# A hand-ordered schedule for two layers of spectral convolution: list offsets of the pairs, the transform back and the first transform

## Chip, cores and metric

One NeuronCore of a Trainium2 chip runs the whole program. The metric is the device time of one execution in microseconds (us), of which smaller is better.

## What is computed

The input `x` is four images of 256 x 256 positions with 64 channels, in float32. Layer 0 is a block with a Fourier branch and a depthwise convolution; layer 1 takes a moving average along the rows and adds a filtered spectrum. Cut to what matters:

```
# layer 0
h  = ln(x) @ w_te + b_te                       # 64 -> 128 channels
F  = fft2(h, axes=(1, 2))
fc = gelu(concat(real(F), imag(F)) @ w_fc + b_fc)
sp = real(ifft2(fc[..., :128] + 1j * fc[..., 128:], axes=(1, 2)))
x1 = x + sp @ w_tp + b_tp
h2 = ln(x1) @ w_fe + b_fe
d  = gelu(depthwise_conv_3x3(h2, w_dw) + b_dw)
x2 = x1 + d @ w_fp + b_fp
# layer 1, along the second axis, for each channel
trend = moving_average(x2, 25)
out   = trend + irfft(einsum(rfft(x2 - trend)[:128], w_real + 1j * w_imag))
```

## The kernel before

Transforms are matmuls with tables of cosines and sines. Layer 0 runs as three streams, and each stream is cut into small operations with short names. The names below are those of the lists; the numbers are lines of the kernel.

**First transform** (`forward_h`, 32 chunks for each image): `fl` loads a chunk (L564, L569), `fq fr fR fm` and `fM fA fB fC fp` are the layer norm's statistics, `fx` scales (L410), `fa fb` fold halves on VectorE (L582, L602), `fh0 fh1` on GpSimd (L609), `y0 y1` are the matmuls (L615), `yt0 yt1` copy out on ScalarE (L633) and write `y_d` to HBM (L649).

**Pairs** (`spectral`, 65 pairs of rows for each image): `x` (L725) is a transform on TensorE that reads `yb` (L680, from `y_d`), `xs` (L740) its copy on ScalarE, `m0 m1` (L750) the channel mix on TensorE, `gc0 gc1` (L764) a copy on ScalarE, `b0 b1` (L770) sum and difference on VectorE, `g0 g1` (L775) the gelu on ScalarE, `p0 p1` (L781) a fold on GpSimd, `z` (L805), `zs` (L813), `w` (L823) and `zt` (L833) a projection, a copy, a transposition and a copy. **Transform back:** `u` (L856, TensorE), `us` (L873, ScalarE), `uc` and `uf` (L887, L888, L907, L920, VectorE), the last with the write of `u_d` (L896). One period has two pairs and one step back.

**Convolution** (`convolution`, 32 chunks for each image): `UL`/`ul` load `uc` from `u_d` (L976, and L985, L997 for an image's first chunk), `c0` (L990) corrects a column, `s` (L1041) is the last transform, `r0 r1` (L1054, L1062) the residual, `cq` to `cp` the second layer norm's statistics (lines as for the first), then transpositions `t`, row sums `T` (L1124 to L1132, GpSimd), the convolution's matmuls `gm gh em eh` (L1166, L1180), its combination, gelu, projection and `st` (L1322).

The order in which TensorE, VectorE, ScalarE and GpSimd get their instructions is written out by hand (`in_order`, L1531). The DMA queue on SyncE is ordered by the framework. Each number `n` is one **period**; the list that belongs to it is walked from the left, and an entry `op:k` asks for operation `op` up to index `n + k` (the stream's own count; pairs count `2 * (n - S0) + k`, `S0` being 35):

```python
    def period(n):
        if any(n - k in chunk_at for k in range(7)):
            names = FULL if n < B * FWD + 4 else MIXED if n < CONV_FROM else CONV
        else:
            names = SPECTRUM
```

`SPECTRUM` has the first transform and the pairs, `FULL` all three streams, `MIXED` the pairs and the convolution, `CONV` the convolution alone. `do(op, index)` first pulls whatever the operation depends on, in the order of that table (`FOLLOWS`), so an index that runs ahead of the last list is made up at that place, one operation after the other:

```python
        for k in range(done.get(op, -1) + 1, index + 1):
            for other, at in EARLY.get(op, ()) if k < LATE_CHUNKS else ():
                do(other, k + at)
            for other, at in follows.get(op, ()):
                do(other, k + at)
```

The convolution's chunks get their periods from `chunk_at` (L1540): image 0 has 71 to 102, image 1 104 to 135, image 2 136 to 167, image 3 169 to 200. `FULL` begins at 71 with `b0:2` and ends with 131; `MIXED` ends with 169. Before an image's first chunk `UL` pulls the last steps back of that image. In `SPECTRUM` a forward chunk's root is a power on GpSimd (L383); in `FULL` it shares a chain of ten small steps with a convolution chunk (`cA` to `cp`, L354 to L397, `rstd_c`), taken in the order ScalarE, GpSimd, ScalarE and so on. After layer 0, layer 1 multiplies with matrices made at the start (L1504).

Of the kernel before, what the change touches and what calls it, by code (L numbers as in the profile page):

```python
# [136 lines left out]
def conv_seq_kernel(ctx: ExitStack, tc: tile.TileContext, a: dict, tables: bass.AP, out: bass.AP):  # L137
    nc = tc.nc
    x = a["x"]
# [11 lines left out]
        x="xs", m0="b0", m1="b1", z="zs", w="zt", u="uc", s="r1", t0="tt0", t1="tt1", gm="cf0",  # L151
        em="ec1", o0="fs0", o1="fs1", ft0="st0", ft1="st1", y0="yt0", y1="yt1",
# [1327 lines left out]
    def x2_load(pool, c, b0, bufs):  # L1480
        xc = pool.tile([P, 2, BH, N // SW, CG, SW], F32, tag="xc", name=f"xc_{c}_{b0}", bufs=bufs)
        for b in range(BH):
            for t in range(2):
                nc.sync.dma_start(
                    xc[:, t, b], x2_d[b0 + b, t * P : (t + 1) * P, c // CG]
                )
        return xc
# [43 lines left out]
    in_order = tc.manual_schedule(engines={ET.PE, ET.DVE, ET.Activation, ET.Pool})  # L1531
    FWD, KH, COLS = P // 4, P // 2 + 1, N // 8
    S0 = FWD + 3
    LATE = 0

    def opened(b):

        return (KH * (b + 1) + 2) // 2 + 1

    chunk_at, at = {}, 0  # L1540
    for b in range(B):
        at = max(at, S0 + opened(b) + 2 + LATE)
        for q in range(COLS):
# [3 lines left out]
    place = {chunk: at for at, chunk in chunk_at.items()}  # L1547
    CONV_FROM = S0 + LATE + opened(B - 1) + 3

# [24 lines left out]
    def numbered(text):  # L1574

        return [(w.split(":")[0], int(w.split(":")[1]) if ":" in w else 0) for w in text.split()]

    follows = {}
    for line in FOLLOWS.replace("\n", "|").split("|"):
# [3 lines left out]


    FULL = numbered("""
        b0:2 ec1:-4 cm:-1 gh:-4 m0:3 gc_0:-4 ec0:-4 a0:-5 cf0:-4 p0:1 g0:2 m1:3 fr:1 fh1:-1 p1:1 z:1
        gc1:3 gc0:3 b1:3 fq:1 o0:-5 fs0:-5 o1:-5 cx:-2 fs1:-5 fh0:-1 b0:3 y0:-1 ft0:-5 g1:2 sp0:-4 w
        st0:-5 zs:1 p0:2 fR:1 fm:1 cc:-1 yt0:-1 ft1:-5 fC:-1 p1:2 fp xl XL t1:-2 ul fM:1 fA st1:-5
        sp1:-4 tt1:-2 s cl t0:-2 w:1 gc_1:-4 tt0:-2 r0 r1 cM:-1 fx T0:-2 T1:-2 z:2 m1:4 gc1:4 fB
        y1:-1 yt1:-1 uf:-1 zs:2 cr UL:1 x:5 xs:5 g0:3 u x:6 b1:4 us m0:4 zt xs:6 gc0:4 zt:1 cf1:-4  # L1590
        fl:2 a1:-4 cA:-1 Ta:-2 cB:-1 cq gm:-3 fa fb cC:-1 cR cp:-1 g1:3 uc em:-3 eh:-3
    """)

    MIXED = numbered("""
        XL:-1 ft0:-6 zs:-3 st0:-6 ft1:-6 st1:-6 em:-4 g0:-1 T1:-3 Ta:-3 eh:-4 zt:-4 ec0:-4 ec1:-4
        m1:-1 sp0:-5 sp1:-5 cx:-2 w:-3 cf1:-5 gc1:-1 g1:-2 b1:-1 cm:-1 cc:-2 UL t0:-2 a0:-5 xs:1
        zt:-3 gm:-4 t1:-2 tt0:-2 a1:-5 p0:-2 p1:-2 z:-2 zs:-2 gh:-4 uf:-2 cM:-1 p0:-1 gc_0:-4 cf0:-4
        g1:-1 cp:-1 m1 gc1 b1 s cl tt1:-2 r0 gc_1:-4 m0 gc0 m0:1 p1:-1 z:-1 gc0:1 r1 x:2 b0 xs:2
        o1:-5 fs1:-5 u:-1 o0:-5 T0:-2 x:3 cq b0:1 us:-1 fs0:-5 g0 cr cR uc:-1 w:-2 ul:1 xl
    """)  # L1600

    CONV = numbered("""
        ce0:-4 ul s cl xl XL r0 ce1:-4 r1 a0:-4 ft0:-5 st0:-5 cr gm:-3 ft1:-5 a1:-4 cq Ta:-2 cR
        o1:-4 o0:-4 gh:-3 st1:-5 t0:-1 gc_0:-3 fs0:-4 gc_1:-3 t1:-1 cm cc:-1 cM cp cf0:-3 tt1:-1
        cf1:-3 tt0:-1 em:-3 eh:-3 T0:-1 T1:-1 cx fs1:-4 UL:1
    """)

    LATE_CHUNKS = CONV_FROM + max(at for op, at in MIXED if op in ("em", "gm"))
# [5 lines left out]
    """)  # L1614

    SPECTRUM = numbered("""
        hm hv fr gc0:-1 x:1 uf:-1 p1:-1 z:-2 m0 xs:1 b0:-1 ht fm UL:1 y1:-2 x fx:-1 zs:-2 y0:-2
        g0:-1 gc0 m1 hc b0 gc1 p1:-1 fR xs w:-2 zt:-2 fb:-1 m0 fq yt1:-2 p0:-1 fp fl:1 XL:1 zs:-1 fM
        z:-1 b1 fa:-1 fh1:-1 u fh0:-1 g0 us uc m1:1 w:-1 b1:1 g1 zt:-1 g1 p0 gc1:1 yt0:-2
    """)  # L1620
    PAIRS = set("x xs m0 m1 gc0 gc1 b0 b1 g0 g1 p0 p1 z zs w zt".split())
    BACK = {"u", "us", "uc", "uf"}
# [54 lines left out]
# [5 lines that stand above are left out]
        joint["on"], joint["whole"] = names is FULL, names is SPECTRUM  # L1682
        for op, at in names:
            base = n
            if op in PAIRS:
                base = 2 * (n - S0)
            elif op in BACK:
                base = n - S0
            elif op in HALF_MATRICES:
                base = (n - S0 - HALF_MATRICES[op]) // 2  # L1690
            do(op, base + at)
# [8 lines left out]
    with in_order, ExitStack() as right:  # L1700
        with (
# [40 lines left out]
            ops |= convolution(conv, pairs)  # L1742
            for n in range(early_end, S0 + LATE + opened(B - 1) + 2):
                period(n)
        with tc.tile_pool(name="seq", bufs=1, side="left", reuse_waits="tile") as seq:
            mts = [matrix_load(seq, c) for c in range(0, CG, CM)]
            xc = x2_load(seq, 0, 0, 1)
            for n in range(S0 + LATE + opened(B - 1) + 2, END):
                period(n)
# [48 lines left out]
```

## Time and profile before

| what | value |
|---|---|
| median of 3 runs | 4370.02 us (4364.57 to 4371.86) |
| the profiled execution | 4357.78 us |
| its span, first to last instruction | 4356.0 us |
| busy: TensorE, VectorE, ScalarE, GpSimd | 4171.1, 3452.7, 2961.9, 3159.4 us |
| one `SPECTRUM` period | 13.6 us |
| one `FULL`, `MIXED`, `CONV` period | 26.9, 23.6, about 14.0 us |
| queue of SyncE and the other hardware queues | 583.84 MB in 726696 packets |

Span and busy times are of one profiled execution, which was 12 us below the median. The lengths of periods are distances between the starts of L1054, which is one VectorE instruction in each chunk of the convolution; in `SPECTRUM` they are distances between copies of `xs` (L740). PE is TensorE, DVE VectorE, ACT ScalarE, POOL GpSimd.

### The profile page before, as it was taken

The numbers are of one execution on the slowest core, as the hardware profiler recorded it, in microseconds if no ns is written. First come the engines' busy times: TensorE is split into PE (matmuls) and PEld (weight loads), VectorE is DVE, ScalarE is ACT, GpSimd is POOL, SyncE is SP. The second block draws the span as 40 slices with busy tenths as digits, with TensorE's granted clock in tenths as the row PEclk, the third lists the DMA queues.
The fourth block names the chain that finished last, engine by engine and source line by source line (L and its number), as shares of the span: only waits on it lengthen the run. The fifth ranks groups of instructions, "written<-read, shape, count | busy, mean of one in ns | idle before, by whom it ended". The sixth has DMA issues, their size and how long they took to land.

```text
span 4356.0 us, 67401 instructions
## 1 busy us (share of the span) xinstructions
PE 4171.1 (96%) x22443; PEld 2320.0 (53%) x22443; DVE 3452.7 (79%) x5234; ACT 2961.9 (68%) x5414; POOL 3159.4 (73%) x3151
## 2 busy tenths in 40 slices
PE   8999999889999999899999989999998799999999
PEld 4544444335555555455555556666665466664444
DVE  7868999679999999899999877888887699972222
ACT  3438998568888888788888777888886466641111
POOL 6869999578888888788888777788887588840000
PEclk9999999889999999999999999999999899999999
DMA  6664555434555544344444333444433544439996
GB/s 192 207 187 141 160 160 163 131 99 128 139 140 139 139 130 135 111 133 136 136 137 130 107 106 95 120 110 110 117 102 89 168 113 112 112 97 370 343 345 230
DMA packets 763907, 655.28 MB, mean 150 GB/s; under 512 B 46414, under 2 KB 657696, under 8 KB 755241
## 3 DMA queue, kind: packets, MB, share of 16 engines
q1 hardware_dynamic: 726696, 583.84, 46.2%
q10 hardware_dynamic: 36864, 67.13, 4.0%
q8 instruction: 180, 2.95, 0.3%
q14 instruction: 167, 1.36, 0.1%
HBM read 364.81 MB, written 286.00 MB: 149 GB/s over the span
## 4 chain that ended last, share of the span: by engine, by line
PE 66%; POOL 12%; DVE 7%; ACT 5%; DMA 5%; issue 4%; SPq 2%; POOLq 0%; ACTq 0%; DVEq 0%
PE ps_o L1504 9%; PE ps_p L750 8%; PE ps_h_c L1166 6%; PE ps_s_c L1041 5%; PE ps_y L615 5%; PE ps_z L805 4%; PE ps_x L725 4%; PE ps_u L856 4%; PE ps_h_c L1180 4%; POOL xb L609 3%; PE ps_f_c L1283 3%; PE ps_hh_c L1166 3%; PE ps_zt L823 3%; PE ps_t_c L1088 3%; POOL g L781 3%
## 5 line engine op out<-in xcount | busy, mean ns | idle before, releaser
L770 DVE TENSOR_TENSOR g<-ps_p,g 128x512 f32<-128x512 f32 x1040 | 701.8, 682 | 152.1 <-ACT g L764 134.0
L781 POOL TENSOR_TENSOR g<-g 128x512 f32<-128x512 f32 (+1 forms) x520 | 675.3, 1309 | 117.1 <-ACT g L775 104.4
L775 ACT ACTIVATE g<-g,b_fc 128x1024 f32<-128x1024 f32 (+1 forms) x520 | 598.1, 1151 | 3.1 <-DVE g L770 3.1
L750 PE MATMUL ps_p<-xs,wp 64*128 64x512 f32 (+1 forms) x2080 | 564.8, 617 | 9.9 <-ACT xs L740 3.8
L1166 PE MATMUL ps_h_c<-td,wc_main 128*128 128x256 f32 x2048 | 516.5, 391 | 6.7 <-DVE g L770 1.4
L764 ACT COPY g<-ps_p 128x512 f32<-128x512 f32 (+1 forms) x520 | 297.7, 584 | 272.9 <-PE ps_z L805 105.0
L1504 PE MATMUL ps_o<-xc,mt 128*128 128x512 f32 x1024 | 441.5, 594 | 1.8 <-DVE oc L1518 1.8
L1166 PEld LDWEIGHTS ps_h_c<-td,wc_main 128*128 128x128 f32 x2048 | 370.5, 193 | 122.2 <-ACT zt L833 39.0
L1276 ACT ACTIVATE h_c<-h_c,b_conv 128x1024 f32<-128x1024 f32 x256 | 297.5, 1163 | 134.0 <-DVE h_c L1245 51.9
L1518 DVE TENSOR_SCALAR oc<-ps_o,b_fp 128x512 f32<-128x512 f32 x128 | 93.5, 749 | 347.7 <-DMA out_dram<-oc 190.4
L1128 POOL TENSOR_TENSOR td<-tt 128x512 f32<-128x512 f32 x256 | 327.0, 1298 | 10.0
L609 POOL TENSOR_TENSOR xb<-xt 128x512 f32<-128x512 f32 x224 | 285.1, 1280 | 64.8 <-DVE xt L602 50.2
L1516 ACT ACTIVATE oc<-ps_o,b_fp 128x512 f32<-128x512 f32 x128 | 86.4, 686 | 359.1 <-PE ps_o L1504 199.2
L1504 PEld LDWEIGHTS ps_o<-xc,mt 128*128 128x128 f32 x1024 | 195.1, 191 | 247.7 <-issue 236.8
L750 PEld LDWEIGHTS ps_p<-xs,wp 64*128 64x128 f32 x2080 | 189.9, 186 | 241.7 <-issue 83.6
L805 PE MATMUL ps_z<-g,w_tp 128*64 128x512 f32 x1024 | 290.9, 619 | 28.3 <-POOL g L781 21.3
L725 PEld LDWEIGHTS ps_x<-tab,yb 128*64 128x64 f32 x4064 | 235.5, 137 | 135.0 <-issue 72.0
L615 PE MATMUL ps_y<-xb,tab 128*64 128x512 f32 x1024 | 274.8, 629 | 28.2 <-POOL xb L609 22.8
L1322 DVE TENSOR_TENSOR st<-x_c,ps_ft_c 128x256 f32<-128x256 f32 x512 | 261.2, 601 | 45.2 <-PE ps_ft_c L1308 41.1
L1180 PE MATMUL ps_h_c<-td,wc_half 64*128 64x256 f32 (+1 forms) x2048 | 279.1, 395 | 3.7 <-POOL td L1132 2.4
L1283 PE MATMUL ps_f_c<-h_c,w_fp 128*64 128x512 f32 x1024 | 265.3, 614 | 16.4 <-ACT h_c L1276 16.4
L1041 PE MATMUL ps_s_c<-uc_c,tab 64*128 64x512 f32 x1024 | 260.7, 616 | 18.3 <-DVE uc_c L990 11.2
(201 smaller groups left out, 9565.4 us busy)
## 6 DMA issues: line engine op xcount, KB each, us to landing
y_d<-yt SPq DMA_DIRECT2D x256, 256.0 KB, 3.4
yb<-y_d SPq DMA_DIRECT2D x256, 256.0 KB, 4.1
u_d<-ut SPq DMA_DIRECT2D x256, 256.0 KB, 3.6
x_c<-in_x_dram SPq DMA_DIRECT2D x512, 128.0 KB, 3.5
x_d<-st SPq DMA_DIRECT2D x128, 512.0 KB, 4.9
xc<-x_d SPq DMA_DIRECT2D x64, 1024.0 KB, 8.3
out_dram<-oc ACTq DMA_DIRECT2D x256, 256.0 KB, 5.9
xt<-in_x_dram SPq DMA_DIRECT2D x504, 128.0 KB, 2.5
```

Of the source, the lines that this page charges most:

```text
L609: engine.tensor_tensor(sums[j][:, i], x0, x1, (ALU.add, ALU.subtract)[i])
L615: nc.tensor.matmul(ps[i * C : (i + 1) * C], dh[:, m, i * C : (i + 1) * C], sums[j][:, i], start=True, stop=True,)
L725: nc.tensor.matmul(ps[r * C : (r + 1) * C, j * N + t * P : j * N + (t + 1) * P], blk[:, t, k, r * C : (r + 1) * C], tb[:, t, :], start=Tru ...
L750: nc.tensor.matmul(ps[:, :nf], wp[rows, cols], rhs[rows], start=True, stop=r == 1 or not pr["special"],)
L770: nc.vector.tensor_tensor(gt[:, i], re, gt[:, 1], op)
L775: nc.scalar.activation(g, g, AF.Gelu, bias=b_fc[:, half : half + 1])
L781: nc.gpsimd.tensor_tensor(g[:, 0], g[:, 0], g[:, 1], op)
L805: nc.tensor.matmul(ps[r * C : (r + 1) * C, :nf], w_tp, d[:, :nf], start=True, stop=True)
L1041: nc.tensor.matmul(pss[i], tb[i * C : (i + 1) * C], uc[i * C : (i + 1) * C, ::-1, 1 - r, :] if down else uc[i * C : (i + 1) * C, :, r, :], ...
L1166: nc.tensor.matmul(product(j, k, par), wc_main[:, par, k, :], td[:, k, slots(j)].rearrange("p j q -> p (j q)"), start=k in (0, 1, 3), stop ...
L1180: nc.tensor.matmul(product(j, k, par)[:, dst.start * Q : dst.stop * Q], wc_half[lo : lo + C, k, :], td[lo : lo + C, k, src].rearrange("p j ...
L1504: nc.tensor.matmul(ps[:, :nf], mts[i // CM][:, i % CM, t, to * P : (to + 1) * P], xc[:, t, :, :, i, :], start=t == 0, stop=t == 1,)
```

## The change

`LATE` goes from 0 to 1, so each chunk of the convolution comes one period later and one more period has the list `SPECTRUM`. In `FULL` the pairs' entries fall by 4 (two periods), those of the transform back and of the first transform by 2; in `MIXED` the pairs' fall by 2 and those of the transform back by 1; in `CONV` everything falls by 1, with `LATE` no move at all. Against the convolution the two other streams are thus one period later in `FULL` and where they were in `MIXED`. Each list is also begun at another operation: what stood at the end of `FULL` (`g1 uc em eh`), of `MIXED` (`xl`) and of `SPECTRUM` (`gc1 yt0`) stands at the front with an index lower by one period.

```diff
...
     in_order = tc.manual_schedule(engines={ET.PE, ET.DVE, ET.Activation, ET.Pool})
     FWD, KH, COLS = P // 4, P // 2 + 1, N // 8
     S0 = FWD + 3
-    LATE = 0
+    LATE = 1
 
     def opened(b):
 
...
 
 
     FULL = numbered("""
-        b0:2 ec1:-4 cm:-1 gh:-4 m0:3 gc_0:-4 ec0:-4 a0:-5 cf0:-4 p0:1 g0:2 m1:3 fr:1 fh1:-1 p1:1 z:1
-        gc1:3 gc0:3 b1:3 fq:1 o0:-5 fs0:-5 o1:-5 cx:-2 fs1:-5 fh0:-1 b0:3 y0:-1 ft0:-5 g1:2 sp0:-4 w
-        st0:-5 zs:1 p0:2 fR:1 fm:1 cc:-1 yt0:-1 ft1:-5 fC:-1 p1:2 fp xl XL t1:-2 ul fM:1 fA st1:-5
-        sp1:-4 tt1:-2 s cl t0:-2 w:1 gc_1:-4 tt0:-2 r0 r1 cM:-1 fx T0:-2 T1:-2 z:2 m1:4 gc1:4 fB
-        y1:-1 yt1:-1 uf:-1 zs:2 cr UL:1 x:5 xs:5 g0:3 u x:6 b1:4 us m0:4 zt xs:6 gc0:4 zt:1 cf1:-4
-        fl:2 a1:-4 cA:-1 Ta:-2 cB:-1 cq gm:-3 fa fb cC:-1 cR cp:-1 g1:3 uc em:-3 eh:-3
+        g1:-3 uc:-3 em:-4 eh:-4 b0:-2 ec1:-4 cm:-1 gh:-4 m0:-1 gc_0:-4 ec0:-4 a0:-5 cf0:-4 p0:-3
+        g0:-2 m1:-1 fr:-1 fh1:-3 p1:-3 z:-3 gc1:-1 gc0:-1 b1:-1 fq:-1 o0:-5 fs0:-5 o1:-5 cx:-2
+        fs1:-5 fh0:-3 b0:-1 y0:-3 ft0:-5 g1:-2 sp0:-4 w:-4 st0:-5 zs:-3 p0:-2 fR:-1 fm:-1 cc:-1
+        yt0:-3 ft1:-5 fC:-3 p1:-2 fp:-2 xl XL t1:-2 ul fM:-1 fA:-2 st1:-5 sp1:-4 tt1:-2 s cl t0:-2
+        w:-3 gc_1:-4 tt0:-2 r0 r1 cM:-1 fx:-2 T0:-2 T1:-2 z:-2 m1 gc1 fB:-2 y1:-3 yt1:-3 uf:-3 zs:-2
+        cr UL:1 x:1 xs:1 g0:-1 u:-2 x:2 b1 us:-2 m0 zt:-4 xs:2 gc0 zt:-3 cf1:-4 fl a1:-4 cA:-1 Ta:-2
+        cB:-1 cq gm:-3 fa:-2 fb:-2 cC:-1 cR cp:-1
     """)
 
     MIXED = numbered("""
-        XL:-1 ft0:-6 zs:-3 st0:-6 ft1:-6 st1:-6 em:-4 g0:-1 T1:-3 Ta:-3 eh:-4 zt:-4 ec0:-4 ec1:-4
-        m1:-1 sp0:-5 sp1:-5 cx:-2 w:-3 cf1:-5 gc1:-1 g1:-2 b1:-1 cm:-1 cc:-2 UL t0:-2 a0:-5 xs:1
-        zt:-3 gm:-4 t1:-2 tt0:-2 a1:-5 p0:-2 p1:-2 z:-2 zs:-2 gh:-4 uf:-2 cM:-1 p0:-1 gc_0:-4 cf0:-4
-        g1:-1 cp:-1 m1 gc1 b1 s cl tt1:-2 r0 gc_1:-4 m0 gc0 m0:1 p1:-1 z:-1 gc0:1 r1 x:2 b0 xs:2
-        o1:-5 fs1:-5 u:-1 o0:-5 T0:-2 x:3 cq b0:1 us:-1 fs0:-5 g0 cr cR uc:-1 w:-2 ul:1 xl
+        xl:-1 XL:-1 ft0:-6 zs:-5 st0:-6 ft1:-6 st1:-6 em:-4 g0:-3 T1:-3 Ta:-3 eh:-4 zt:-6 ec0:-4
+        ec1:-4 m1:-3 sp0:-5 sp1:-5 cx:-2 w:-5 cf1:-5 gc1:-3 g1:-4 b1:-3 cm:-1 cc:-2 UL t0:-2 a0:-5
+        xs:-1 zt:-5 gm:-4 t1:-2 tt0:-2 a1:-5 p0:-4 p1:-4 z:-4 zs:-4 gh:-4 uf:-3 cM:-1 p0:-3 gc_0:-4
+        cf0:-4 g1:-3 cp:-1 m1:-2 gc1:-2 b1:-2 s cl tt1:-2 r0 gc_1:-4 m0:-2 gc0:-2 m0:-1 p1:-3 z:-3
+        gc0:-1 r1 x b0:-2 xs o1:-5 fs1:-5 u:-2 o0:-5 T0:-2 x:1 cq b0:-1 us:-2 fs0:-5 g0:-2 cr cR
+        uc:-2 w:-4 ul:1
     """)
 
     CONV = numbered("""
-        ce0:-4 ul s cl xl XL r0 ce1:-4 r1 a0:-4 ft0:-5 st0:-5 cr gm:-3 ft1:-5 a1:-4 cq Ta:-2 cR
-        o1:-4 o0:-4 gh:-3 st1:-5 t0:-1 gc_0:-3 fs0:-4 gc_1:-3 t1:-1 cm cc:-1 cM cp cf0:-3 tt1:-1
-        cf1:-3 tt0:-1 em:-3 eh:-3 T0:-1 T1:-1 cx fs1:-4 UL:1
+        ce0:-5 ul:-1 s:-1 cl:-1 xl:-1 XL:-1 r0:-1 ce1:-5 r1:-1 a0:-5 ft0:-6 st0:-6 cr:-1 gm:-4
+        ft1:-6 a1:-5 cq:-1 Ta:-3 cR:-1 o1:-5 o0:-5 gh:-4 st1:-6 t0:-2 gc_0:-4 fs0:-5 gc_1:-4 t1:-2
+        cm:-1 cc:-2 cM:-1 cp:-1 cf0:-4 tt1:-2 cf1:-4 tt0:-2 em:-4 eh:-4 T0:-2 T1:-2 cx:-1 fs1:-5 UL
     """)
 
     LATE_CHUNKS = CONV_FROM + max(at for op, at in MIXED if op in ("em", "gm"))
...
     """)
 
     SPECTRUM = numbered("""
-        hm hv fr gc0:-1 x:1 uf:-1 p1:-1 z:-2 m0 xs:1 b0:-1 ht fm UL:1 y1:-2 x fx:-1 zs:-2 y0:-2
-        g0:-1 gc0 m1 hc b0 gc1 p1:-1 fR xs w:-2 zt:-2 fb:-1 m0 fq yt1:-2 p0:-1 fp fl:1 XL:1 zs:-1 fM
-        z:-1 b1 fa:-1 fh1:-1 u fh0:-1 g0 us uc m1:1 w:-1 b1:1 g1 zt:-1 g1 p0 gc1:1 yt0:-2
+        gc1:-1 yt0:-3 hm hv fr gc0:-1 x:1 uf:-1 p1:-1 z:-2 m0 xs:1 b0:-1 ht fm UL:1 y1:-2 x fx:-1
+        zs:-2 y0:-2 g0:-1 gc0 m1 hc b0 gc1 p1:-1 fR xs w:-2 zt:-2 fb:-1 m0 fq yt1:-2 p0:-1 fp fl:1
+        XL:1 zs:-1 fM z:-1 b1 fa:-1 fh1:-1 u fh0:-1 g0 us uc m1:1 w:-1 b1:1 g1 zt:-1 g1 p0
     """)
     PAIRS = set("x xs m0 m1 gc0 gc1 b0 b1 g0 g1 p0 p1 z zs w zt".split())
     BACK = {"u", "us", "uc", "uf"}
```

## Prediction, made before the run

> **What bounds the kernel now.** First the page: TensorE is busy almost throughout, and its clock falls where it is not.
>
> ```profile
> PE 4171.1 (96%) x22443; PEld 2320.0 (53%) x22443; DVE 3452.7 (79%) x5234; ACT 2961.9 (68%) x5414; POOL 3159.4 (73%) x3151
> PE   8999999889999999899999989999998799999999
> PEclk9999999889999999999999999999999899999999
> ```
>
> Each of the 40 slices is 108.9 us. The weak ones are, counted from 0, 7 and 8 (762 to 980 us), 16 (from 1742), 23 (from 2505), 30 and 31 (3267 to 3485). Next I took the starts of L1054, one for each chunk of the convolution, which give the length of each period, and asked for busy times in exactly these stretches. The columns are stretch, length, busy PE, PEld, DVE, ACT, POOL, granted clock, DMA share, GB/s.
>
> ```profile
> 795.70:809.30 13.60, 12.84 (x76) 5.00 (x74) 13.21 (x18) 11.41 (x21) 13.16 (x8) 1.00 0.85 229
> 809.30:866.00 56.70, 39.00 (x146) 14.92 (x146) 19.91 (x28) 24.00 (x39) 21.83 (x16) 0.70 0.31 86
> 866.00:889.30 23.30, 20.90 (x113) 8.99 (x113) 19.08 (x30) 14.11 (x24) 10.18 (x7) 0.93 0.34 93
> 889.30:915.50 26.20, 20.59 (x85) 8.15 (x86) 16.45 (x23) 16.10 (x31) 14.40 (x14) 0.80 0.28 86
> 915.50:943.20 27.70, 21.23 (x97) 8.55 (x98) 20.66 (x24) 17.98 (x35) 22.04 (x18) 0.82 0.35 96
> 1052.40:1079.20 26.80, 26.63 (x162) 14.68 (x161) 24.98 (x38) 22.78 (x45) 23.62 (x23) 1.00 0.43 118
> ...
> 2440.20:2469.20 29.00, 25.80 (x153) 14.68 (x152) 23.64 (x35) 20.28 (x38) 19.05 (x20) 1.00 0.27 73
> 2469.20:2496.10 26.90, 26.60 (x157) 15.20 (x156) 20.69 (x32) 20.62 (x40) 18.89 (x20) 1.00 0.36 98
> 2496.10:2517.70 21.60, 20.16 (x120) 11.74 (x120) 16.56 (x23) 16.94 (x35) 14.39 (x23) 1.00 0.35 98
> 2517.70:2540.50 22.80, 16.65 (x82) 12.03 (x82) 14.00 (x21) 9.48 (x18) 16.85 (x24) 0.85 0.43 115
> ```
>
> The first line is the last `SPECTRUM` period and 1052 a full `FULL` period: TensorE leaves under 0.8 us of either. Between them lies the hole: 56.7 us from the start of period 71 to its residual `r0`, with 39.0 us of TensorE at 0.70 of the clock, which is 27 us of work. After it the convolution's pipeline fills, and periods 72 to 75 take 23.3 to 27.7 us though they hold less than a full one. The last lines are the end of `FULL` and the start of `MIXED`. The waits from 811 to 866 us, longest in total first, say what the hole is:
>
> ```profile
> DVE g L770 <- ACT g L764: 26.0, 7, 7.9
> POOL g L781 <- ACT g L775: 21.2, 5, 7.2
> POOL xb L609 <- DVE xt L602: 10.5, 1, 10.5
> PEld ps_z L805 <- POOL g L781: 8.9, 5, 2.9
> ```
>
> Here each engine waits for the one before it in a pair's own chain. The timeline there shows it instruction by instruction, with idle time and releaser in brackets:
>
> ```profile
> 820.53 1.13 PE L750 MATMUL ps_p<-xs,wp 64*128 64x512 f32 x4
> ...
> 832.84 0.58 ACT L740 COPY xs<-ps_x 128x512 f32<-128x512 f32 x1 [5.71 <-PE ps_p L750]
> ...
> 835.04 1.27 POOL L781 TENSOR_TENSOR g<-g 128x512 f32<-128x512 f32 x1 [7.23 <-ACT g L775]
> ...
> 836.50 1.42 DVE L770 TENSOR_TENSOR g<-ps_p,g 128x512 f32<-128x512 f32 x2 [7.92 <-ACT g L764]
> ```
>
> `FULL` asks at once for `b0:2`, `m0:3` and then `x:5`, `x:6`, where `SPECTRUM` ended with `x:1`. So the list's first entry pulls whole pairs, one behind the other: seven `x` in period 71 instead of two. By 847 us four L750 matmuls take 3.5 us instead of the 1.13 above.
>
> **What the skill says.** The Trainium skill, "TensorE: Matmul & The Clock Gate", section "What's actually happening", says that a gate halves TensorE's clock after an idle window of about 3.4 us and restores it after a busy one. The trace agrees in kind: from 837.8 to 851.2 us the granted clock was 0.53. "Trainium Architecture — The Big Picture", section "Inside one NeuronCore": each engine has its own instruction stream, and they meet only at semaphores. That is the pattern of these waits: one late copy stops everything queued behind it.
>
> **The change, part by part.** All in the profiled execution's time: span 4356.0 us, 1.8 us around it, 12.2 us under the median of the runs.
>
> (1) *One more `SPECTRUM` period, and no jump.* After the change the first `FULL` period is 72. Its entries `b0:-2`, `m0:-1`, `p0:-3` and so on were already reached; new are three `x` (74 to 76), four L750 groups, one `z`, and the chunk's `s`. In the two built programs' instruction order `s` follows straight on the last L750 of `SPECTRUM`; before, four `x` and eight groups of L750 with all that they pull stand between. So from 809.3 us: 13.6 for the added period and 2.0 from the start of `s` to that of L1054 (941.2 to 943.2 us in period 74), 15.6 in place of 56.7: **-41**. The load of `uc` isn't in the way: its source is written by `uf` at the head of period 71, 1.4 us of VectorE, 3.6 us to land and as much to load, some 9 of the 13.6 us. Bounds: -46 (the clock stays full and period 71 is shorter without the power chain behind it) to -30 (`uc` late by a landing or two).
>
> (2) *Period 72 to 73.* Before 23.3 us at clock 0.93. After, it lacks the first transform (`fl` to `y` pause for one period) and, in 73, the root chain of a chunk before it, whose wait on GpSimd was 7.9 us. I take 21: **-2**, from -6 to +2.
>
> (3) *The rest of the filling, periods 73 to 77* (before 26.2, 27.7, 27.5, 27.8, 27.0): held by the chain of ScalarE and GpSimd steps that roots and folds share, which stays in the same order. **0**, from -6 to +8.
>
> (4) *Steady periods.* In both programs a `FULL`, `MIXED` or `CONV` period has the same cyclic order of operations on every engine, and the same order of loads and stores on SyncE's queue apart from a few periods at image boundaries: **0**. The root powers (L383) go from 75 to 74.
>
> (5) *Work put off.* At equal chunks the new order is two pairs and one forward chunk behind. From the timeline a pair costs TensorE about 4.9 us (`x` 0.9, two L750 groups 2.3, `z` 1.1, transposition 0.6), `y` 1.9: 12 us. It lands where `FULL` ends, in the room that the table shows: 29.0 - 25.8, 21.6 - 20.2 and 22.8 - 16.7, about 11 us. There the old lists stop the pairs for more than a period (`x:6` to `x:3`), the new ones for half of one (`x:2` to `x:1`). Against it, one period of 26.9 becomes one of 23.6. I price +12 of work less 9 hidden less 3.3: **0**, from -5 to +6.
>
> (6) *Boundary of image 1.* In 104 (new) `UL` pulls two steps back at once, before it was one: VectorE has 2 x (1.36 + 1.3) = 5.3 us in a row (L887 and L888, then L920 or L907), with `us` in a single buffer, and behind them `g0`, `b1` of the pairs, for which `p0` and `z` wait; on SyncE four `u_d` writes stand ahead of the image's first load and of `yb`. The load has some 15 us of slack (issued at 1738.7 us, needed by L990 at 1757.4). **+3**, from 0 to +8. Images 2 and 3 keep their order.
>
> Sum: -41 - 2 + 3 = **-40**: a span of 4316, an execution of 4318 where the profiled one took 4357.8, and 4330 against the median of 4370.
>
> **Rivals.** About 0.2% (9 us) is what a measurement of this kernel can tell from no change.
>
> *Half the gain* (0.13): the filling needs the pairs' lead. Before, pairs are two ahead while the convolution starts; without it periods 73 to 77 wait for the fold (L781) that holds `z` for 14.3 us in all from 893 to 950 us. Four us in each of five periods: -20, 4350. Against it: the pull order is the same one.
>
> *More* (0.08): with the clock never halved, the filling runs at the 20 to 21 us that TensorE needs, five times 3 us: -55, 4315.
>
> *Slower* (0.05): the period gets longer. The new lag changes which forward chunk shares a root with which convolution chunk; where they don't meet, GpSimd does a power of 2.9 us (L383) in every `FULL` period, and 23.6 + 2.9 leaves nothing of 26.8. This decides from 0.67 us in each of 60 periods (40 us); with 1 us it gives 4390. Against it: the count of L383 falls.
>
> *It doesn't do what it says* (0.03): the hole belongs to the change of pools and to the first load from `u_d`, not to the jump; then one `SPECTRUM` period is added (+13.6) and one `FULL` becomes `MIXED` (-3.3): 4380. Against it: no such wait among the long ones.
>
> **Numbers.** The likeliest case, 0.71, gives 4330 with 4318 to 4343 of its own. The range must reach the half gain: 4311 to 4354. Faster 0.89 (the first three cases, less 0.03 for a half gain that is nearly none), within 0.2% 0.03, slower 0.08.
>
> **What would show it.** After, slices 7 and 8 read 9 in PE and the clock; the distance from the last `SPECTRUM` copies to the first L1054 is about 16 us after one more period's start, not 57; full periods stay at 26.9 and 23.6. The step would be wrong if the first `s` waits for `uc`, if the filling takes over 28 us a period, or if `FULL` is longer than 26.9.

## The result: 4322.9 us in place of 4369.5, and the profile after

The changed kernel takes **4322.9 us** (median of 4 runs, 4319.8 to 4325.4), the kernel before 4369.5 on the same chip (4 runs): ratio **0.9894**, 95% interval 0.9877 to 0.9912, or 46.6 us less. The profiled execution took 4325.4 us, its span 4323.6.

The page of the changed kernel: busy time of the engines, and busy TensorE and granted clock in 40 slices, now of 108.1 us.

```profile
PE 4158.0 (96%) x22443; PEld 2315.2 (54%) x22443; DVE 3453.4 (80%) x5234; ACT 2961.5 (68%) x5409; POOL 3163.4 (73%) x3156
PE   8999999899999999899999999999998899999999
PEclk9999999989999999999999999999999999999999
```

The work is the same (22443 matmuls, TensorE busy 13 us less). Slice 7 (757 to 865 us) still reads 8 in TensorE and slice 8 (865 to 973 us) 8 in the clock: one of the two weak slices of the start is left in each row. Slice 31 reads 8 where it read 7.

The stretches of the changed kernel, with the columns of the table before: the added `SPECTRUM` period, what follows up to the first L1054, three periods of filling, a full one.

```profile
805.50:819.10 13.60, 12.67 (x73) 4.97 (x70) 11.10 (x16) 11.02 (x20) 13.37 (x9) 1.00 0.72 204
819.10:826.50 7.40, 4.97 (x14) 1.63 (x12) 2.89 (x6) 2.36 (x4) 2.08 (x2) 0.68 0.70 213
826.50:848.10 21.60, 17.71 (x99) 7.76 (x98) 15.29 (x25) 11.98 (x20) 6.89 (x5) 0.95 0.25 73
848.10:875.00 26.90, 20.18 (x75) 8.67 (x76) 15.27 (x21) 15.62 (x30) 12.12 (x12) 0.68 0.23 66
875.00:902.10 27.10, 21.58 (x98) 8.83 (x98) 19.76 (x23) 17.99 (x35) 21.11 (x18) 0.81 0.28 78
1011.20:1038.10 26.90, 26.70 (x162) 14.74 (x161) 25.07 (x38) 22.85 (x45) 23.74 (x23) 1.00 0.42 118
```

Of the hole of 56.7 us 7.4 us are left: at 826.5 us the first L1054 starts, where it started at 866.0. The full period is 26.9 us as before. What has not changed is the filling: 26.9 and 27.1 us with TensorE busy for 20.2 and 21.6 of them, at a clock of 0.68 and 0.81.

To place every gain and loss, here are the distances in us between fixed points of the program, for all kernels of this study. The points are the last `xs` copy (L740) of period 70 and the starts of L1054 of the named chunks (image, number); the last column goes to the end of the last L1516, some 4.5 us before the end of the span. The stretch to (1,6) holds the start of image 1, that to (2,1) the end of `FULL` and the start of image 2, that to (3,2) the start of image 3 and of `CONV`. Up to that first point all programs are the same, so the first column (794.7 to 802.3) shows how far executions of one and the same order scatter.

| kernel | start to L740 | to (0,0) | to (0,1) | to (0,6) | to (0,31) | to (1,6) | to (2,1) | to (2,31) | to (3,2) | to the end |
|---|---|---|---|---|---|---|---|---|---|---|
| before | 798.5 | 67.5 | 23.3 | 136.1 | 676.1 | 229.1 | 709.4 | 707.4 | 89.3 | 914.7 |
| before_again | 798.1 | 67.6 | 23.3 | 136.2 | 676.7 | 231.9 | 709.5 | 709.0 | 94.0 | 913.4 |
| after | 794.7 | 31.8 | 21.5 | 136.3 | 676.3 | 235.2 | 712.5 | 707.2 | 83.1 | 920.5 |
| late_only | 799.3 | 84.6 | 23.3 | 136.0 | 676.1 | 224.9 | 703.8 | 705.6 | 93.8 | 915.2 |
| lists_only | 798.9 | 17.2 | 20.4 | 133.5 | 676.4 | 233.1 | 719.8 | 707.5 | 89.4 | 915.5 |
| late_two | 799.1 | 44.1 | 20.5 | 135.2 | 676.1 | 229.1 | 705.9 | 706.0 | 83.1 | 916.9 |
| half_jump | 797.9 | 34.1 | 22.6 | 133.2 | 675.6 | 235.5 | 713.6 | 707.5 | 84.1 | 917.7 |
| old_conv | 801.1 | 30.0 | 20.5 | 135.2 | 676.3 | 235.1 | 712.4 | 707.3 | 93.8 | 919.6 |
| back_early | 796.3 | 30.0 | 20.5 | 135.1 | 675.8 | 233.3 | 712.0 | 707.7 | 83.5 | 914.3 |
| forward_kept | 799.7 | 32.9 | 20.8 | 135.0 | 678.1 | 234.0 | 710.0 | 707.5 | 81.5 | 917.1 |
| begun_elsewhere | 800.1 | 72.9 | 26.6 | 136.9 | 676.5 | 230.1 | 711.8 | 704.5 | 92.3 | 915.0 |
| ramp | 797.8 | 18.6 | 31.7 | 201.7 | 675.6 | 231.1 | 709.3 | 707.0 | 91.0 | 914.0 |
| ramp_conv | 802.3 | 18.3 | 32.0 | 201.1 | 675.7 | 231.8 | 709.2 | 707.1 | 83.0 | 916.1 |
| ramp_slow | 796.4 | 18.4 | 31.9 | 167.6 | 715.8 | 229.6 | 711.4 | 707.2 | 93.9 | 916.7 |

The change itself, in the first and third row: -35.7 and -1.8 at the start, nothing in the rest of the filling and in the full periods, +6.1 at image 1, +3.1 from there to (2,1), -6.2 where `CONV` begins, +5.8 in the last column. With the 3.8 us by which this execution was early at L740 they make the -32.4 us between the two spans.

### The profile page after: what moved, and what is told of

Read it like the earlier page. It is cut to its first block, busy times and chain, and to the rows that moved or that the text cites. A ratio compares the mean times of both kernels' runs of the same rounds, so it can differ in the third digit from the quotient of the medians.

```text
span 4323.6 us, 67389 instructions
## 1 busy us (share of the span) xinstructions
PE 4158.0 (96%) x22443; PEld 2315.2 (54%) x22443; DVE 3453.4 (80%) x5234; ACT 2961.5 (68%) x5409; POOL 3163.4 (73%) x3156
## 4 chain that ended last, share of the span: by engine, by line
PE 42%; POOL 6%; DVE 4%; DMA 4%; ACT 3%; issue 1%; SPq 1%; ACTq 0%; POOLq 0%; DVEq 0%
PE ps_o L1504 9%; PE ps_h_c L1166 5%; PE ps_p L750 3%; PE ps_s_c L1041 3%; PE ps_h_c L1180 3%; PE ps_f_c L1283 3%; PE ps_hh_c L1166 2%; PE ps_z L805 2%; PE ps_t_c L1088 2%; PE ps_u L856 2%; PE ps_x L725 2%; PE ps_ft_c L1308 2%; DMA out_dram<-oc 1%; PE ps_zt L823 1%; POOL xb L609 1%
## 5 line engine op out<-in xcount | busy, mean ns | idle before, releaser
L770 DVE TENSOR_TENSOR g<-ps_p,g 128x512 f32<-128x512 f32 x1040 | 702.2, 683 | 127.9 <-ACT g L764 109.7
L750 PE MATMUL ps_p<-xs,wp 64*128 64x512 f32 (+1 forms) x2080 | 561.1, 615 | 9.9 <-DVE g L770 2.7
L1516 ACT ACTIVATE oc<-ps_o,b_fp 128x512 f32<-128x512 f32 x128 | 86.2, 686 | 363.0 <-PE ps_o L1504 196.7
L750 PEld LDWEIGHTS ps_p<-xs,wp 64*128 64x128 f32 x2080 | 189.3, 186 | 239.6 <-issue 84.7
L805 PE MATMUL ps_z<-g,w_tp 128*64 128x512 f32 x1024 | 288.7, 617 | 24.6 <-POOL g L781 19.9
L615 PE MATMUL ps_y<-xb,tab 128*64 128x512 f32 x1024 | 273.4, 623 | 23.3 <-POOL xb L609 17.1
```

What stands on the lines that cost most here:

```text
L750: nc.tensor.matmul(ps[:, :nf], wp[rows, cols], rhs[rows], start=True, stop=r == 1 or not pr["special"],)
L770: nc.vector.tensor_tensor(gt[:, i], re, gt[:, 1], op)
L805: nc.tensor.matmul(ps[r * C : (r + 1) * C, :nf], w_tp, d[:, :nf], start=True, stop=True)
```

## The experiments

Theory: the hole is the jump of the pairs, pulled one behind the other; taking the jump away is the gain, and the added `SPECTRUM` period is its price. Rivals: the convolution only began too soon; it matters where the lists begin; the loss at image 1 and the gain at `CONV` have causes of their own. Ratios are those of the timed runs against the kernel before on the same chip.

### The period alone, the lists alone

`late_only`:

```diff
-    LATE = 0
+    LATE = 1
```

> The four old lists with LATE = 1: the SPECTRUM period is added, the jump of the pairs stays (seven x in period 72). Theory (the jump makes the hole): the first FULL period is 57 us long as before, the added period comes on top with 13.6 us and one FULL period becomes a MIXED one (-3.3): before + 10, about 4380 us. Rival (the convolution only begins too soon, its first load or the new pools are late, and one period more hides that): the hole shrinks to 16 us with the old lists too, about 4330 us.

Measured: 4369.9 us (13 runs), ratio 1.0008 (0.9999 to 1.0016). The stretches of this kernel, the added period and the first `FULL` one:

```profile
810.10:823.70 13.60, 12.67 (x73) 4.93 (x70) 11.10 (x16) 11.02 (x20) 13.37 (x9) 1.00 0.72 206
823.70:883.90 60.20, 42.39 (x149) 16.53 (x148) 21.01 (x30) 24.72 (x39) 21.20 (x15) 0.66 0.20 61
```

The hole stands behind the added period with its whole length, 60.2 us at a clock of 0.66. So the convolution was not merely early, and the pools and the first load are not the cause. But the kernel is not 10 us slower either: of the 17.1 us that it loses at the start it gets most back, at image 1 (224.9 in place of 229.1 and 231.9) and on the way to (2,1) (703.8 in place of 709.4).

`lists_only`, against the changed kernel (the four lists stay new; the bounds for the pools and the end of `MIXED` keep their values):

```diff
-    LATE = 1
+    LATE = 0
-    CONV_FROM = S0 + LATE + opened(B - 1) + 3
+    CONV_FROM = S0 + 1 + opened(B - 1) + 3
```

> The new lists with LATE = 0 (chunks stand where they stood; the two bounds in which LATE stood for the pools and the end of MIXED keep their new values). No SPECTRUM period is added and nothing jumps in period 71 (three x), but UL pulls three back steps at image 1 and two each at images 2 and 3, where the changed kernel pulls two, one and one. Theory: against the changed kernel -13.6 for the period, +3.3 for one FULL in place of a MIXED, +6 for each of the three more back steps by the 6.3 us that the one at image 1 cost: +8, 4331 us, from 4318 to 4345. Rival (back steps pulled at once are hidden, the 6.3 us at image 1 have another cause): -10, 4313 us.

Measured: 4321.1 us, ratio 0.9894 (0.9881 to 0.9908), the same as the changed kernel. **The lists alone bring the whole gain.** From the start of the first `FULL` period up to the first L1054, and the period after:

```profile
809.70:816.10 6.40, 3.53 (x11) 1.41 (x12) 1.98 (x5) 1.51 (x4) 2.68 (x3) 0.73 1.00 289
816.10:836.50 20.40, 16.57 (x98) 7.28 (x97) 15.19 (x24) 11.98 (x20) 6.89 (x5) 1.00 0.43 126
```

So the hole goes with the jump alone, without a period more. The kernel is 14.6 us ahead of the changed one at (0,0), and in the timed runs nothing of that is left: it loses 7.3 us on the way to (2,1) (719.8 in place of 712.5) and 6.3 on the way to (3,2) (89.4 in place of 83.1). My price of 6 us for each further step back was too high: from the last chunk of an image to the first of the next it is 1.4 us slower than the changed kernel before image 1, 3.6 before image 2 and 4.2 before image 3.

`late_two` carries the row on, against the changed kernel:

```diff
-    LATE = 1
+    LATE = 2
```

> The new lists with LATE = 2: one SPECTRUM period more than in the changed kernel, and only one back step is left to pull at image 1. Theory (the added period costs its 13.6 us at the start and comes back at the image boundaries and at the end of FULL, where LATE = 1 gave 12 us with the old lists): +2 against the changed kernel, 4325 us, from 4319 to 4331. Rival (the changed kernel has taken what there is to be had there): +13, 4336 us.

Measured: 4322.2 us, ratio 0.9903 (0.9888 to 0.9918). The start is 12.3 us longer than in the changed kernel, image 1 is 6.1 and the stretch to (2,1) 6.6 us shorter. So the new lists with `LATE` at 0, 1 and 2 give 0.9894, 0.9894 and 0.9903. A period's work done ahead is paid for at the start and saved later; in this kernel, where TensorE is busy 96% of the time, it comes to nothing.

### How the hole grows with the jump

`half_jump`, against lists_only (the same in `MIXED`):

```diff
-        ... b0:-2 ... m0:-1 ... fr:-1 ... x:1 ... u:-2 ... x:2 ...
+        ... b0 ... m0:1 ... fr ... x:3 ... u:-1 ... x:4 ...
```

> As lists_only (LATE = 0), but pairs two places, first transform and back steps one place further ahead in FULL and MIXED, so that each stands to its chunk as in the changed kernel and half of the jump is left: five x in period 71, where lists_only has three and the kernel before seven. Theory (the hole grows with the pairs that are pulled; the four that before has more than lists_only cost 55 us, 14 each): +28 against lists_only, less some 10 us that it gains at the boundaries: 4338 us, from 4328 to 4350. Rival (any jump makes the whole hole, since it is one serial chain with the clock halved once): 4360 us or above. Rival (the first two pairs find idle engines): 4320 us or below.

Measured: 4330.3 us, ratio 0.9924 (0.9911 to 0.9936). From L740 to (0,6) it takes 189.9 us, lists_only 171.1, the kernel before 226.9. So the first two pairs that are pulled, with a chunk of the first transform and a step back that come along, cost 18.8 us, and the next two, with as much beside them, 37.0: not one fixed hole, and more than in proportion. The changed kernel has done the same pairs, chunks and steps as half_jump by (0,6), and takes 189.6 us. So the first half of the jump costs no more than an added period that has places for these pairs; it is the second half that makes the loss.

`ramp` takes the old lists and spreads the jump over five periods:

```diff
-            base = n
+            base = n - (names is FULL and n < min(chunk_at) + 4) * (op in forward)
             if op in PAIRS:
-                base = 2 * (n - S0)
+                base = 2 * (n - S0) - max(0, min(chunk_at) + 4 - n) * (names is FULL)
```

> The old lists and LATE = 0, but in the first four periods of FULL the pairs stand 4, 3, 2 and 1 places back (three x in each of periods 71 to 75 in place of seven in 71) and the first transform one chunk back. So the jump is spread, no period is added, and from period 75 on the order is that of the kernel before. Theory (the hole is the jump, the pairs' lead is worth having later): the first chunks as in lists_only, which stood 55 us ahead at chunk (0,6), less 0 to 20 us for four pairs of 4.9 us of TensorE that are now done while the convolution fills, of which its idle time there hides most; image boundaries as in the kernel before. About 4312 us, from 4303 to 4328. Rival (the filling is held by ScalarE and GpSimd, every pair put there costs its whole 5 us and more): 4330 us or above.

Measured: 4388.2 us, ratio 1.0052 (1.0040 to 1.0065): slower than the kernel before (4365.7 us there), where I had expected 4312 and the rival 4330 or above. The stretches from (0,1) on, each with one pair more than its list has places for (the last has a chunk more of the first transform too):

```profile
848.10:884.90 36.80, 24.37 (x116) 9.57 (x116) 19.21 (x28) 20.82 (x38) 16.68 (x16) 0.91 0.23 71
884.90:925.50 40.60, 27.48 (x130) 11.16 (x129) 23.76 (x27) 23.22 (x44) 26.82 (x22) 0.92 0.23 65
925.50:985.30 59.80, 38.67 (x186) 19.06 (x184) 29.13 (x37) 24.90 (x48) 31.51 (x27) 0.80 0.25 71
```

In lists_only the first two of these periods take 25.7 and 26.9 us. So a pair that is worth 4.9 us of TensorE makes its period 11 us (with a step back that lists_only doesn't have there) and 14 us longer, though TensorE was idle for 5 to 7 us there. The waits from 848 to 986 us, longest in total first, say why:

```profile
DVE g L770 <- ACT g L764: 31.4, 12, 6.2
POOL newton_c L355 <- ACT newton_c L354: 21.5, 3, 11.7
PEld ps_z L805 <- POOL g L781: 19.7, 8, 5.2
POOL g L781 <- ACT g L775: 18.7, 6, 5.9
```

It is the picture of the old hole: a pair's own chain, engine after engine. The second line is of the root chain of small steps between ScalarE and GpSimd, so the rival, that these two hold the filling, may have its part. TensorE's idle time while the convolution fills was no room for these pairs: a pair without places of its own in the list is pulled at one place, and all four engines wait through its chain in order. With the same pairs, chunks and steps done by (0,6) as in the kernel before, ramp needs 252.0 us from L740 to there, the kernel before 226.9. That the pull order does it, and not the first transform's shifted place, is argued from these waits; no run here separates them.

`ramp_slow` makes up one place in every second period; against ramp:

```diff
-            base = n - (names is FULL and n < min(chunk_at) + 4) * (op in forward)
+            base = n - (names is FULL and n < min(chunk_at) + 8) * (op in forward)
             if op in PAIRS:
-                base = 2 * (n - S0) - max(0, min(chunk_at) + 4 - n) * (names is FULL)
+                base = 2 * (n - S0) - max(0, min(chunk_at) + 8 - n) // 2 * (names is FULL)
```

> As ramp, but one place made up in every second period, so eight periods, three x in 71, 72, 74, 76 and 78. Theory (TensorE's idle time while the convolution fills hides the pairs): periods 76 to 79 are full ones with TensorE never idle, so one or two of the four pairs cost their 4.9 us there: 3 to 10 us over ramp. Rival (the filling is held by ScalarE and GpSimd): 3 to 10 us under ramp.

Measured: 4399.0 us, ratio 1.0078 (1.0064 to 1.0092). From (0,0) to (0,31) it needs 915.3 us, ramp 909.0 and lists_only 830.3: the pairs cost as much in full periods as in filling ones.

`begun_elsewhere` is the kernel before with three lists, `FULL`, `MIXED` and `SPECTRUM`, begun as the new ones are (`SPECTRUM` is the new one):

```diff
     FULL = numbered("""
-        b0:2 ec1:-4 ... cp:-1 g1:3 uc em:-3 eh:-3
+        g1:1 uc:-1 em:-4 eh:-4 b0:2 ec1:-4 ... cp:-1
     MIXED = numbered("""
-        XL:-1 ft0:-6 ... ul:1 xl
+        xl:-1 XL:-1 ft0:-6 ... ul:1
```

> The kernel before with its lists only begun at the operations at which the new ones begin (indices of the moved entries brought to the period), all distances as before, LATE = 0. Theory (only the distances count): within 3 us of the kernel before, 4367 to 4373 us. Rival (where the list begins decides what the first FULL period pulls first): 10 to 40 us faster.

Measured: 4373.2 us, ratio 1.0011 (1.0005 to 1.0018). A little slower: the first two `FULL` periods take 8.7 us more. With the old distances, no part of the gain lies in what a list begins with.

### Where CONV begins

`old_conv`, against the changed kernel:

```diff
-        ce0:-5 ul:-1 s:-1 cl:-1 xl:-1 XL:-1 r0:-1 ce1:-5 r1:-1 a0:-5 ft0:-6 ...
+        ce0:-4 ul s cl xl XL r0 ce1:-4 r1 a0:-4 ft0:-5 ...
```

> The changed kernel with the old list CONV (s:0 and so on), so that at the change from MIXED to CONV the convolution's later steps jump by one period again. Theory (the new CONV takes away a second, smaller jump, which the prediction left out): +5 to +7 against the changed kernel, 4328 to 4330 us, and the loss lies in the three periods from chunk (3,0) on. Rival (the shorter distance there comes from the later pairs, not from the list): within 2 us of the changed kernel, 4323 us.

Measured: 4335.0 us, ratio 0.9926 (0.9914 to 0.9939), 12 us over the changed kernel. The two periods from (3,0), first in old_conv, then in the changed kernel:

```profile
3365.90:3388.20 22.30, 16.63 (x75) 10.43 (x76) 15.27 (x26) 7.45 (x12) 6.11 (x7) 0.88 0.90 319
3388.20:3411.70 23.50, 19.38 (x93) 12.30 (x94) 18.24 (x36) 8.23 (x17) 9.12 (x24) 0.87 0.47 142
```

```profile
3363.50:3383.30 19.80, 16.83 (x87) 9.91 (x86) 16.73 (x28) 7.81 (x14) 10.20 (x18) 0.97 0.85 300
3383.30:3398.60 15.30, 14.25 (x82) 10.03 (x82) 15.02 (x34) 7.89 (x16) 5.16 (x13) 1.00 0.84 250
```

45.8 us against 35.1, all of what the stretch to (3,2) differs by. The new list alone does that; why, I read from the lists. The old `MIXED` ends with the convolution's late steps at `ft0:-6`, `em:-4`, and the old `CONV` begins with `ft0:-5`, `em:-3`: a second, smaller jump, in which two chunks' late steps fall into one period. The new `CONV` continues `MIXED` without one. The account of the change ahead of the prediction is wrong on this: it says that with `LATE` everything in `CONV` keeps its place. Against `MIXED`, whose convolution entries did not move, it comes one period later.

`ramp_conv`, against ramp:

```diff
-        ce0:-4 ul s cl xl XL r0 ce1:-4 r1 a0:-4 ft0:-5 ...
+        ce0:-5 ul:-1 s:-1 cl:-1 xl:-1 XL:-1 r0:-1 ce1:-5 r1:-1 a0:-5 ft0:-6 ...
```

> As ramp, with the new list CONV too. Theory (the old CONV makes the convolution's later steps jump by a period at the start of CONV, whatever the pairs do): 6 to 13 us under ramp, 4300 to 4306 us if ramp gives 4312. Rival (that jump costs only beside the later pairs of the new lists, where it cost 12 us): within 2 us of ramp.

Measured: 4383.0 us, ratio 1.0043 (1.0030 to 1.0055), 5 us under ramp; the stretch to (3,2) is 83.0 in place of 91.0 us. So the gain there doesn't hang on the later pairs; the intervals of the two kernels overlap, the stretch settles it. In all kernels it is 81.5 to 84.1 us with the new `CONV` and 89.3 to 94.0 with the old one, but for lists_only, whose 89.4 us have in them the 4.2 us of one step back more before image 3.

### The rest

`back_early`, against the changed kernel, at the end of period 103:

```diff
             do(op, base + at)
+        if n == 103:
+            do('us', n - S0 - 1)
```

> The changed kernel, but the first of the two back steps that UL pulls in period 104 is done at the end of period 103, so that one is left. Theory (the 6.3 us lost at image 1 are the two back steps in a row): chunk (1,0) and those after it 4 to 6 us earlier, 4317 to 4319 us. Rival (the loss is the time from the last back step's store to the chunk's load, or lies with TensorE): within 1.5 us of the changed kernel, 4323 us.

Measured: 4322.9 us, ratio 0.9900 (0.9887 to 0.9914). Image 1 takes 233.3 us in place of 235.2. The second of the two back steps did wait in the changed kernel, though not for `us`, as the prediction has it, but for `ut`, whose write to `u_d` had to land (columns: start, duration, then the idle time and its releaser):

```profile
1697.71 0.69 DVE L887 TENSOR_TENSOR ut<-ps_u,us 128x512 f32<-128x512 f32 x1 [2.71 <-DMA u_d<-ut]
```

but taking it out of there brings 2 us of the loss, not 4 to 6. late_two, with one more `SPECTRUM` period of lead, has none of it (229.1).

`forward_kept` moves the first transform's entries of `FULL`, and only those, up by 1:

```diff
-        ... fr:-1 fh1:-3 ... fq:-1 ... y0:-3 ... fl ...
+        ... fr fh1:-2 ... fq ... y0:-2 ... fl:1 ...
```

> The changed kernel, with the first transform one place further ahead in FULL, so that it stands to the convolution as in the kernel before and doesn't pause in period 72. Theory (the first transform has no part in the jump with LATE = 1): within 3 us of the changed kernel, 4320 to 4326 us. Rival (its pause is what lets the convolution start so quickly): the first two FULL periods together 5 to 10 us longer, 4328 to 4333 us.

Measured: 4326.0 us, ratio 0.9913 (0.9900 to 0.9927). The first two periods take 53.7 us, in the changed kernel 53.3: the pause has no part in the quick start. The interval reaches that of the changed kernel, so whether this move is worth the last 3 us is open.

`before_again` is the kernel before, profiled a second time.

> The kernel before once more, unchanged, for a second profile. The profile of before lies 12 us under the median of its runs. If that is chance in the hole (in begun_elsewhere and late_only the first FULL period was some 3 to 6 us longer than in it), this profile has a span of 4360 to 4368 us and its first FULL period is 58 to 66 us long; if it is chance elsewhere, that period is 56 to 57 us again and the rest differs.

Measured: span 4364.0 us. The same stretches as above, hole, image 1 and the two periods from (3,0):

```profile
809.00:865.60 56.60, 38.91 (x145) 14.82 (x146) 19.79 (x28) 23.90 (x38) 21.74 (x16) 0.70 0.32 88
1701.80:1764.90 63.10, 54.65 (x311) 30.77 (x309) 50.43 (x72) 44.86 (x86) 49.91 (x45) 0.93 0.46 129
3400.30:3422.70 22.40, 16.72 (x75) 10.41 (x76) 15.31 (x27) 7.45 (x12) 6.14 (x7) 0.88 0.92 321
```

The hole is 56.6 us again; what differs lies at image 1 (60.3 us at a clock of 0.99 in the first profile) and behind (3,0) (20.8 us at 0.96), each time with the clock lower. The changed kernel's span is 40.4 us shorter than this one. That is not to be set against the 46.6 us of the timed runs: this profile belongs to another set of runs, in which the kernel before took 4364.2 us (median of 9) in place of 4369.5, and the profiled execution of the changed kernel was 2.5 us above its median. In its last stretch, 920.5 us, the changed kernel has the order of back_early, which took 914.3: there too one order scatters by 6 us.

No version here is faster than the changed kernel by more than its interval.

## Why the prediction held, and where its steps did not

Forecast 4330 us (4311 to 4354), measured 4322.9; the likeliest case, that the jump makes the hole, is the one that the runs confirm. Step by step, from the first profiles of the two kernels:

| step | predicted | measured | |
|---|---|---|---|
| (1) period added, no jump | -41 (-46 to -30) | -35.7 | in its bounds, a wait left out |
| (2) period 72 to 73 | -2 | -1.8 | right |
| (3) the rest of the filling | 0 | +0.2 | right |
| (4) steady periods | 0 | +0.2, -0.2 | right |
| (5) work put off | 0 (-5 to +6) | +3.1 | in its bounds |
| (6) image 1 | +3 (0 to +8) | +6.1, or +3.3 to the second profile | size in bounds, mechanism only in part |
| `CONV` | not priced | -6.2, or -10.9 to the second profile | left out |

**(1)** The 13.6 us for the added period were right. What was mis-sized is what comes after it: 2.0 us from the start of `s` to L1054, with `s` straight behind the last L750. It took 7.4 us. The chain there in the changed kernel, TensorE and VectorE:

```profile
818.75 1.55 PE L750 MATMUL ps_p<-xs,wp 64*128 64x512 f32 x4
...
821.01 1.42 DVE L770 TENSOR_TENSOR g<-ps_p,g 128x512 f32<-128x512 f32 x2 [0.56 <-ACT g L764]
822.34 0.28 DVE L990 TENSOR_TENSOR uc_c<-uc_c,first 128x128 f32<-128x128 f32 x1
...
822.73 3.79 PE L1041 MATMUL ps_s_c<-uc_c,tab 64*128 64x512 f32 x8 [2.43 <-issue]
```

The load of `uc` was early enough, as predicted (issued at 801.5 us). But the image's first column is corrected on VectorE by L990, and that stands behind the last pair's L770, which waits for a copy of the last L750. So TensorE is idle for 2.43 us before `s`. The trace names no releaser, but `s` starts 0.1 us after L990 ends, and in late_two, old_conv and back_early the gap is 2.4 us too. This wait was in no term of the sum. Then L1054 starts 3.8 us after `s`, at a granted clock of 0.50; in those three kernels it starts 2.0 us after it, as predicted, at full clock. back_early and old_conv, which have the same order up to there, take 30.0 in place of 31.8 us: the 1.8 us are the clock, and chance. The price of a period at the start was about right too (14.6 and 12.3 us for `LATE` from 0 to 1 and from 1 to 2); that it comes back later was in no step.

**(5)** The sign of the balance was open, and the row of `LATE` gives it a slope: 719.8, 712.5 and 705.9 us in the stretch to (2,1) for the new lists with 0, 1 and 2, some 7 us for a period of lead, against 709.4 before. Only part of that is the end of `FULL`. From the last chunk of image 1 to (2,1) it is 58.3, 55.5 and 51.5 us: there lists_only pulls two steps back, the changed kernel one, late_two none.

**(6)** was priced by the two back steps in a row. back_early shows that the row is about 2 us of it. But back_early only moves the step to a place a little ahead of the same chunk, and what goes with the time is how many steps are done between the last chunk of image 0 and the first of image 1. Counted by their writes to `u_d` (L896, two for a step), with the distance of the two L1054:

| writes of `u_d` | kernels | us |
|---|---|---|
| 4 | late_only | 55.3 |
| 6 | before, before_again, late_two, begun_elsewhere, ramp, ramp_conv, ramp_slow | 60.3 to 63.1 |
| 8 | after, half_jump, old_conv, back_early, forward_kept | 67.1 to 68.2 |
| 10 | lists_only | 69.6 |

The changed kernel has one step more there than the kernel before, so the step named was the right one, and its price of 3 us was low. Through which wait a step back delays the chunk is open. The clock in that stretch is 0.93 in the changed kernel and in the second profile of before, 0.99 in the first.

**CONV** was missed because I read the move of all its entries by 1 as the move of `LATE`, and didn't lay `MIXED` and `CONV` side by side as I had `SPECTRUM` and `FULL`. It helped: -6 to -11 us, about what (1), (5) and (6) lacked. The sum of -40 came out near the measured -46.6 by such an exchange, and so in part by luck, not by each term being right.

**The rivals.** *Half the gain* falls with 136.3 us of filling against 136.1: the pairs' lead was no use there. *More* falls too: full clock at the start doesn't last. In period 73 TensorE's gap in front of L805 is there as before, and the clock goes with it:

```profile
863.68 1.97 PE L805 MATMUL ps_z<-g,w_tp 128*64 128x512 f32 x2 [3.90 <-POOL g L781]
```

Two of these matmuls take 1.97 us here and four take 1.08 at 875.96, with the clock at 0.50 from 864 to 872 us. The Trainium skill, "TensorE: Matmul & The Clock Gate", section "What's actually happening", gives an idle window of about 3.4 us for that, and this gap of 3.90 us agrees. *Slower* falls with full periods of 26.9 us. *It doesn't do what it says* falls with late_only, where the hole moves along with the jump, and with lists_only, where it goes without an added period. Of the signs named beforehand one was wrong: slices 7 and 8 don't both read 9, because they hold this filling. The first L1054 came 21.0 us after the added period's start, not 16.

## What to carry to other kernels

In an order written out by hand, lay the lists on both sides of every change of list beside each other: where an operation's distance grows from one to the next, the steps that are missing are pulled at one place, as a chain in which all engines wait for one another. Two pairs with a chunk and a step back take 13.6 us in a `SPECTRUM` period of their own; here the first two that were pulled cost 18.8 us, the next two 37.0, and spreading the four over several periods cost more still. In this kernel, starting the later list with the distances at which the earlier one stops was worth more than the lead that the jump bought.

## What was not expected of the hardware

Executions of one order differ by several us in places where TensorE has gaps of some 2 to 4 us, and the granted clock differs with them: the same two periods from (3,0) took 43.0 and 45.9 us in the kernel before, at clocks of 0.92 to 0.96 and of 0.87 to 0.88. A gap shorter than the 3.4 us named above can be enough: after 2.36 us without a matmul (846.96 to 849.32 us in the changed kernel) the clock was 0.50 from 849.3 to 855.0 us, and after a like gap in old_conv 0.65 for the 4 us that followed. A single profile was up to 12 us off the median, and the medians of the kernel before in four sets of runs, three of them on different chips, lie between 4364.2 and 4369.5 us. So a gain of 1% is better read against more than one profile, and within one set of runs.
